# Gated cross-attention block: softmax issued two steps ahead, the work behind it regrouped, and one PSUM tile for each chunk of the first layer

## Chip, cores, metric

One core of one Trainium2 chip. The metric is the device time of one launch in microseconds (us), as the median of several runs.

## What is computed

`x` is 4096 rows of 512 floats. It passes two residual stages.

```
q = layernorm(x) Wq^T + bq          k, v = ctx Wk^T + bk, ctx Wv^T + bv      (ctx: 2 x 77 rows)
a = softmax(q k^T / sqrt(32))       16 heads of 32
x = x + tanh(g0) * (concat(a v) Wo^T + bo)
n = layernorm(x);  h = gelu(quant(n) quant(w1)^T + b1 ...)      512 -> 2048
x = x + tanh(g1) * (quant(h) quant(w2)^T + b2 ...)              2048 -> 512
```

`quant` rounds to whole numbers with one scale for the whole tensor, the largest absolute value over 127. So no row of the first layer can start before every row's second layernorm is known, and no row of the second before every value of `h` is.

## The kernel before

The rows form 8 blocks (`NB`) of 512, each of 4 row tiles of 128. All `x` stays in SBUF (`X[i]`). There are three stages.

**Attention** (lines 409 to 501). Block `i` has 8 steps `s`: a step is one group of four heads (`g = s // 2`) and one half of the rows. The helpers, with the names that the profile shows:

- `project_q` (line 245): 4 matmuls into `pq`; ACT copies to `qT`.
- `softmax` (258): 4 matmuls into `ps` (two row groups of the array side by side); DVE takes the maximum `mx` (276) and subtracts into `e` (280); ACT takes exp (286); DVE sums (288) and inverts (290); POOL multiplies (291).
- `transpose_a` (297): 4 PE transposes of `e` into `pta`; ACT copies to `aT` (305).
- `apply_v` (307): 4 matmuls of 32 columns each into `pc`, side by side in four column groups of the array; ACT copies to `cT` (321).
- `project_o` (323): 4 matmuls into `po` over the four `cT`; DVE adds into `X` (333).
- `norm` and `transpose_x` (222, 229) prepare the next block: `xn` on DVE, `ptx` on PE, `xnT` on ACT.
- `norm2_stats`, `norm2_max` (337, 342): the second layernorm's statistics, and the largest value of a block.
- `weight_step` (386): in blocks 1 to 4, DVE finds the largest weight and quantizes w1 and w2.

In step `s` the code issues the softmax of step `s + 1`, the two transposes of step `s`, and other pieces at fixed steps. Here PE's order isn't written out by hand: a scheduler orders each engine's instructions by its own model of the times, starting from the source, and may put matmuls of one group between those of another. Each engine then runs its list in order, with semaphores between engines. `tc.issue_after` puts a group behind a given instruction; `manual_schedule` keeps the source's order on the engines that it names.

`e` has 3 buffers; `ps`, the transposes' tile `pt` (for `pta` and `ptx`) and the tile `pp` (for `pq`, `pc` and `po`) have 2 each in PSUM.

**Between the stages** (493 to 569). After the last `project_o`, the last tile's layernorm gives the last maximum; `scale_of` (148) turns the maxima into one scale by a small matmul (`pg_x`). Block 0 is normalized for the first layer by POOL (`normalize_x(0, nc.gpsimd)`, line 563, tile `xs`), quantized and transposed through `px` to `xqT`.

**First layer** (570 to 611). Each block has 16 chunks (`fc`) of 128 hidden units, of 4 matmuls each. Two chunks share one PSUM tile `ph` of two banks, and there are two such tiles; the waits go by the tile. ACT applies Gelu to a chunk (590), DVE takes the largest value of two chunks (600). The next block is normalized, quantized and transposed (`xs`, `xq`, `px`, `xqT`) within the same loop. `G` goes to DRAM for six blocks and stays in SBUF for two.

**Second layer** (623 to 665): quantize `G`, 64 matmuls a block into `pf`, add, write out. The change leaves it alone.

Of the kernel before, what the change touches and what calls it, by code (L numbers as in the profile page):

```python
# [8 lines left out]
F32 = mybir.dt.float32  # L9
# [33 lines left out]
def tile_flamingo_gated_block(  # L43
# [50 lines left out]
    bv_sb = awts.tile([NK, D], F32, name="bv_sb")  # L94
# [5 lines left out]
    b2_sb = const.tile([P, D], F32, name="b2_sb")  # L100
# [17 lines left out]
    nc.sync.dma_start(b2_sb, b2.to_broadcast([P, D]))  # L118
# [10 lines left out]
    w1q = const.tile([P, KC, FF], BF16, name="w1q")  # L129
    w2q = const.tile([P, FC, D], BF16, name="w2q")  # L130
# [33 lines left out]

    def quantize(dst, src, inv):
# [8 lines left out]
    with actx:  # L174
        work = actx.enter_context(tc.tile_pool(name="work", bufs=2))
# [4 lines left out]
        kblk, vblk = [], []  # L180
        for b in range(B):
            kb = awts.tile([P, NG, RK], F32, name=f"kb{b}")
            nc.gpsimd.memset(kb, 0.0)
            kblk.append(kb)
            vblk.append(awts.tile([NK, D], F32, name=f"vb{b}"))
# [56 lines left out]
        def add_bias(i, t):  # L242
            nc.gpsimd.tensor_tensor(X[i][:, t, :], X[i][:, t, :], bo_sb, ALU.add)
# [98 lines left out]
        def norm2_max(i, t0=0, t1=NT):  # L342

            tm = small.tile([P, NT], F32, tag="tm", name=f"tm{i}_{t0}")
            for t in range(t0, t1):
                xn = work.tile([P, D], F32, tag="xn", name=f"xf{i}_{t}")
                nc.vector.tensor_scalar(
                    xn,
                    X[i][:, t, :],
                    mean2[:, i, t, 0:1],  # L350
                    rstd2[:, i, t : t + 1],
                    ALU.subtract,
                    ALU.mult,
                )
# [4 lines left out]
            nc.vector.tensor_reduce(xmax[:, k : k + 1], tm[:, : t1 - t0], AX.X, ALU.max)  # L359
# [67 lines left out]
        softmax(0, 0)  # L427
        for i in range(NB):
            for s in range(2 * NG):
                last = None  # L430
                if s + 1 < 2 * NG:
                    last = softmax(i, s + 1)
                    last_product = last["POOL"]
                elif i + 1 < NB:
                    last = softmax(i + 1, 0)
                transpose_a(i, s, 0)

                if i == 0 and s < 2:
# [36 lines left out]
                if s == 7 and i > 0:  # L475
                    norm2_stats(i - 1)
                    norm2_max(i - 1)
                if last is not None:
                    with tc.issue_after(last["DVE"]):
                        weight_step(i, s)  # L480
                    t = s - NT if i == 0 else s // 2
                    if t >= 0 and (i == 0 or s % 2 == 0):
                        with tc.issue_after(last["POOL"]):
                            add_bias(i, t)
# [23 lines left out]
    )  # L508

    def gtile(name):  # L510
        return gpool.tile([P, GF, TB], F32, tag="G", name=name)

# [4 lines left out]
    with ExitStack() as fctx:  # L517
        fwork = fctx.enter_context(tc.tile_pool(name="fwork", bufs=2, reuse_waits="tile"))
        ps_h = fctx.enter_context(
            tc.tile_pool(name="ps_h", bufs=2, space=PSUM, reuse_waits="tile")  # L520
# [5 lines left out]
        def normalize_x(i, engine):  # L526
            xs = fwork.tile([P, NT, D], F32, tag="xs", name=f"xs{i}")
            for t in range(NT):
                engine.tensor_scalar(
                    xs[:, t, :],  # L530
                    X[i][:, t, :],
                    mean2[:, i, t, 0:1],
                    rstd2[:, i, t : t + 1],
                    ALU.subtract,
                    ALU.mult,
                )
            return xs

        def quantize_x(i, xs, n):
# [3 lines left out]
            for t0 in range(0, NT, n):  # L543
                v, vq = xs[:, t0 : t0 + n, :], xq[:, t0 : t0 + n, :]
                if n == 1 and t0 >= NT // 2:
                    nc.scalar.activation(v, v, AF.Copy, bias=MAGIC, scale=inv_x)
                    last = nc.vector.tensor_scalar(vq, v, MAGIC, None, ALU.subtract).ins
                else:
                    last = quantize(vq, v, inv_x)
                for t in range(t0, t0 + n):  # L550
                    px = ps_x.tile([P, KC, P], BF16, tag="px", name=f"px{i}_{t}")
                    for kc in range(KC):
                        nc.tensor.transpose(px[:, kc, :], xq[:, t, kc * P : (kc + 1) * P], identb)
                    dst = xqT[:, :, t * P : (t + 1) * P]
                    if n == 1:
                        nc.scalar.copy(dst, px)  # L556
                    else:
                        nc.vector.tensor_copy(dst, px)
            return xqT, last
# [9 lines left out]
        nc.vector.tensor_scalar(b1s, b1_sb, s1, None, ALU.mult)  # L569
        for i in range(NB):  # L570
            cur = xqT
            if i + 1 < NB:
                with tc.issue_after(last):
                    xs = normalize_x(i + 1, nc.vector)
                xqT, last = quantize_x(i + 1, xs, NT)
            for a in range(GT):
                G = gtile(f"G{i}_{a}")
                for v in range(GF // 2):
                    ph = ps_h.tile([P, 2, TB], F32, tag="ph", name=f"ph{i}_{a}_{v}")
                    for u in range(2):  # L580
                        fc = a * GF + 2 * v + u
                        for kc in range(KC):
                            nc.tensor.matmul(  # L583
                                ph[:, u, :],
# [7 lines left out]
                            ph[:, u, :],  # L592
# [135 lines left out]
```

## Time and profile before

| | |
|---|---|
| median of 3 runs | 720.01 us (718.1 to 720.77) |
| the profiled execution, its own time | 718.17 us |
| its span, first to last instruction | 716.2 us |
| mean granted PE clock | 0.986 of full |
| busy: PE, DVE, ACT, POOL | 662.0, 526.9, 345.7, 210.7 us |
| attention, PE's first `ps` to last `po` | 22.5 to 443.1 us |
| from there to the first matmul of layer one | to 457.6 us |
| layer one, PE | 457.6 to 584.2 us |
| rest | to 716.2 us |

A row of a timeline has a start, a length (both in us from the span's start), the engine, the line, the operation, what it writes and reads, and a count of like instructions merged. In brackets stands how long its engine was idle before it and who ended that. The ends of matmuls are modelled and overlap what follows, so for PE the distance from start to start is the true cost. A float matmul shows as two records.

### The profile page before, as it was taken

To read this page: it belongs to the slowest core of one execution; us is meant where nothing else is said; L and a number is where in the kernel's file an instruction comes from. 1 tells how busy PE (TensorE), PEld (TensorE's weight loads), DVE (VectorE), ACT (ScalarE), POOL (GpSimd) and SP (SyncE) were. 2 spreads that over 40 slices of the span, in tenths; PEclk is the share of its full clock that TensorE was granted. 3 is DMA by queue.
4 is the path that set the end of the run, shared out by engine and by line. 5 is a ranking of instruction groups with operands and counts; after the bars stand their busy time and mean duration, and the time that the engine had idled before them with its cause. 6 is when DMAs were issued, how large, how long until landed. Compare 5 with 4: busy or idle time off the path is not lost.

```text
span 716.2 us, 8398 instructions
## 1 busy us (share of the span) xinstructions
PE 662.0 (92%) x3160; PEld 326.6 (46%) x3160; DVE 526.9 (74%) x821; ACT 345.7 (48%) x474; POOL 210.7 (29%) x164
## 2 busy tenths in 40 slices
PE   4998999899999999999999997699999978999977
PEld 2655445445445445454555543344444433444433
DVE  3564678889888799587577668799997669855542
ACT  2455344334344334444444440477777779454540
POOL 2134323234232342432333232300000009991000
PEclk9999999999999999999999999699999999999999
DMA  9900200121311311100000000066666107699871
GB/s 300 343 1 11 107 0 1 37 82 59 118 59 59 119 59 59 59 1 0 1 1 0 1 1 0 22 271 259 271 265 264 59 0 293 249 346 335 329 253 74
DMA packets 26432, 85.44 MB, mean 119 GB/s; under 512 B 3531, under 2 KB 3531, under 8 KB 20248
## 3 DMA queue, kind: packets, MB, share of 16 engines
q1 hardware_dynamic: 24520, 83.54, 31.0%
q10 hardware_dynamic: 1872, 1.37, 0.6%
q8 instruction: 25, 0.41, 0.2%
q14 instruction: 15, 0.12, 0.0%
HBM read 51.34 MB, written 33.55 MB: 119 GB/s over the span
## 4 chain that ended last, share of the span: by engine, by line
PE 58%; DVE 21%; DMA 7%; POOL 6%; ACT 4%; issue 3%; SPq 1%; POOLq 0%; DVEq 0%; ACTq 0%
PE ph L583 17%; PE pq L248 9%; PE po L326 8%; PE pf L645 7%; PE pta L304 6%; DMA Gb<-h 6%; PE ps L267 4%; POOL e L291 3%; DVE mx L276 3%; PE pc L313 3%; DVE sm L288 2%; DVE e L280 2%; DVE st_a L141 2%; ACT Gb L636 1%; DVE st_f L141 1%
## 5 line engine op out<-in xcount | busy, mean ns | idle before, releaser
L291 POOL TENSOR_TENSOR e<-e,rs 128x616 f32<-128x616 f32 x64 | 77.9, 1218 | 261.7 <-DVE rs L290 190.2
L583 PE MATMUL ph<-xqT,w1q 128*128 128x512 bf16 x512 | 124.2, 381 | 0.9 <-ACT xqT L556 0.7
L645 PE MATMUL pf<-w2q,hq 128*128 128x512 bf16 x512 | 114.4, 386 | 9.4 <-DVE hq L637 4.9
L248 PE MATMUL pq<-xnT,wq_sb 128*128 128x512 f32 x256 | 121.0, 613 | 0.9 <-ACT xnT L240 0.9
L305 ACT COPY aT<-pta 77x512 f32<-77x512 f32 x128 | 73.5, 580 | 93.7 <-PE pta L304 93.6
L326 PE MATMUL po<-wo_sb,cT 128*128 128x512 f32 x256 | 117.5, 597 | 0.0
L590 ACT ACTIVATE G<-ph,b1s,s 128x512 f32<-128x512 f32 x128 | 99.5, 777 | 28.9 <-PE ph L583 23.8
L659 POOL TENSOR_TENSOR x<-x,b_sb 128x512 f32<-128x512 f32 x32 | 57.9, 1853 | 135.6 <-DVE b_sb L616 135.6
L304 PE MATMUL pta<-ident,e 128*77 128x128 f32 x512 | 81.2, 284 | 13.8 <-POOL e L291 11.0
L304 PEld LDWEIGHTS pta<-ident,e 128*77 128x77 f32 x512 | 57.7, 147 | 68.1 <-POOL e L291 33.7
L600 DVE TENSOR_REDUCE hmax<-G 128x1 f32<-128x1024 f32 (+1 forms) x65 | 75.2, 1196 | 16.4 <-ACT G L590 16.1
L645 PEld LDWEIGHTS <-hq 128*128 128x128 bf16 x512 | 50.4, 99 | 73.2 <-issue 8.3
L583 PEld LDWEIGHTS <-w1q 128*128 128x128 bf16 x512 | 49.2, 97 | 67.6 <-issue 18.2
L276 DVE TENSOR_REDUCE mx<-ps 128x8 f32<-128x616 f32 x64 | 50.2, 786 | 39.9 <-PE ps L267 39.6
L248 PEld LDWEIGHTS pq<-xnT,wq_sb 128*128 128x128 f32 x256 | 46.7, 194 | 53.2 <-issue 50.2
L636 ACT ACTIVATE Gb<-Gb,inv_h 128x2048 f32<-128x2048 f32 x24 | 47.6, 1999 | 46.3 <-DMA Gb<-h 46.3
L288 DVE TENSOR_REDUCE sm<-e 128x8 f32<-128x616 f32 x64 | 50.4, 789 | 25.0 <-ACT e L286 24.4
L286 ACT ACTIVATE e<-e 128x616 f32<-128x616 f32 x64 | 45.8, 716 | 42.6 <-DVE e L280 42.5
L326 PEld LDWEIGHTS po<-wo_sb,cT 128*128 128x128 f32 x256 | 45.6, 190 | 45.0 <-issue 44.5
L637 DVE TENSOR_SCALAR hq<-Gb 128x2048 bf16<-128x2048 f32 x24 | 36.9, 1547 | 32.2 <-ACT Gb L636 32.2
L267 PE MATMUL ps<-kb,qT 64*128 64x154 f32 x512 | 55.5, 319 | 0.9 <-ACT qT L256 0.8
L256 ACT ACTIVATE qT<-pq,bq_sb 128x512 f32<-128x512 f32 x32 | 22.0, 687 | 65.5 <-PE pq L248 65.5
(90 smaller groups left out, 646.5 us busy)
## 6 DMA issues: line engine op xcount, KB each, us to landing
h<-G SPq DMA_DIRECT2D x24, 1024.0 KB, 3.8
Gb<-h SPq DMA_DIRECT2D x24, 1024.0 KB, 7.2
raw_w<-in_w2T SPq DMA_DIRECT2D x8, 1024.0 KB, 5.0
out_y<-x SPq DMA_DIRECT2D x32, 256.0 KB, 3.8
x<-in_x SPq DMA_DIRECT2D x7, 1024.0 KB, 5.0
raw_w<-in_w1T SPq DMA_DIRECT2D x4, 1024.0 KB, 9.8
x<-in_x SPq DMA_DIRECT2D x4, 256.0 KB, 6.2
wq_sb<-in_wqT ACTq DMA_DIRECT2D x1, 1024.0 KB, 10.6
```

The costliest lines, as they stand in the source:

```text
L248: nc.tensor.matmul(pq, wq_sb[:, kc, g * P : (g + 1) * P], xnT[i][:, kc, :], start=(kc == 0), stop=(kc == KC - 1),)
L267: nc.tensor.matmul(ps[:, q, u * RK : (u + 1) * RK], qT[i, g][r, t * P : (t + 1) * P], kblk[i // NBB][r, g, :], start=True, stop=True,)
L276: nc.vector.tensor_reduce(mx, sc, AX.X, ALU.max)
L288: nc.vector.tensor_reduce(sm, e4, AX.X, ALU.add)
L291: last["POOL"] = nc.gpsimd.tensor_tensor(e4, e4, rs[:, :, :, None].to_broadcast([P, 2, HG, NK]), ALU.mult).ins
L304: nc.tensor.transpose(pt[:NK, j, :], es[i, s][:, u, j, :], ident)
L305: nc.scalar.copy(aT[i, g][:, :, t * P : (t + 1) * P], pt[:NK, :, :])
L326: nc.tensor.matmul(po, cT[i, g][:, t * P : (t + 1) * P], wo_sb[:, g, :], start=(g == 0), stop=(g == NG - 1),)
L583: nc.tensor.matmul(ph[:, u, :], w1q[:, kc, fc * P : (fc + 1) * P], cur[:, kc, :], start=(kc == 0), stop=(kc == KC - 1),)
L590: nc.scalar.activation(G[:, 2 * v + u, :], ph[:, u, :], AF.Gelu, bias=b1s[:, fc : fc + 1], scale=s1,)
L600: nc.vector.tensor_reduce(hmax[:, k + u : k + u + 1], G[:, 2 * v + u : 2 * v + u + n, :], AX.XY, ALU.max, apply_absolute_value=True,)
L645: nc.tensor.matmul(po[t], hq[:, fc, t * P : (t + 1) * P], w2q[:, fc, :], start=(fc == 0), stop=(fc == FC - 1),)
```

## The change

- The softmax is issued two steps ahead in place of one: two softmaxes and one more `project_q` before the loop, and step `s` issues that of `s + 2`.
- The pieces of a step stand at other steps. `apply_v` of the group before and `project_o` of the block before come at even steps, one behind the other (before: 2, 4, 6, 0 and 1, 3, 5, 6). `project_q` comes at 1 and 3 for the groups 2 and 3, and at 5 and 7 for groups 0 and 1 of the next block. `norm` goes from step 3 to step 1, `transpose_x` from 5 and 6 to 3 and 5.
- Block 0's normalization for the first layer moves from POOL, after the attention, to DVE in step 5 of the last block (`xs0`, in a buffer of `aT`). Its quantization and transposition stand in the attention's pools (`xq0`, `xqT0`), with two of the four copies on DVE. The last tile's `norm2_max` is kept behind the one before it.
- First layer: each chunk has its own `ph` of one bank, with four of them, and PE keeps the source's order. The 16 transposes of the next block's `xq` stand together ahead of the last four chunks of a block.
- The load of `b2` moves from the start to after the attention; `bv_sb` moves to a buffer of `cT`.

```diff
-        softmax(0, 0)
+        softmax(0, 0)
+        softmax(0, 1)
+        project_q(0, 1)
         for i in range(NB):
             for s in range(2 * NG):
-                last = None
-                if s + 1 < 2 * NG:
-                    last = softmax(i, s + 1)
-                    last_product = last["POOL"]
+                if s + 2 < 2 * NG:
+                    last = softmax(i, s + 2)
                 elif i + 1 < NB:
-                    last = softmax(i + 1, 0)
+                    last = softmax(i + 1, s + 2 - 2 * NG)
                 transpose_a(i, s, 0)
...
-                if s == 0:
-                    if i > 0:
-                        apply_v(i - 1, NG - 1)
-                    project_q(i, 1)
...
-                if s in (2, 4):
-                    project_q(i, 1 + s // 2)
-                    apply_v(i, s // 2 - 1)
-                if s in (1, 3, 5, 6) and i > 0:
-                    project_o(i - 1, (1, 3, 5, 6).index(s))
-                if s == 6:
-                    apply_v(i, 2)
+                if s % 2 == 0:
+                    if s > 0:
+                        apply_v(i, s // 2 - 1)
+                    elif i > 0:
+                        apply_v(i - 1, NG - 1)
+                    if i > 0:
+                        project_o(i - 1, s // 2)
+                if s in (1, 3):
+                    project_q(i, (s + 3) // 2)
                 if i + 1 < NB:
-                    if s == 3:
+                    if s == 1:
                         with tc.issue_after(last["DVE"]):
                             norm(i + 1)
-                    if s in (5, 6):
-                        for t in (2 * s - 10, 2 * s - 9):
+                    if s in (3, 5):
+                        for t in (s - 3, s - 2):
                             transpose_x(i + 1, t)
                 transpose_a(i, s, 1)
-                if s == 6 and i + 1 < NB:
-                    project_q(i + 1, 0)
+                if s in (5, 7) and i + 1 < NB:
+                    project_q(i + 1, (s - 5) // 2)
...
+                with tc.issue_after(last["DVE"]):
+                    weight_step(i, s)
+                    if i == NB - 1 and s == 5:
+                        xs0 = work.tile([P, NT, D], F32, tag="aT", name="xs0", bufs=3)
+                        for t in range(NT):
+                            normalize2(xs0[:, t, :], 0, t)
...
-                    norm2_max(NB - 1, t - 1, t)
-        norm2_max(NB - 1, NT - 1, NT)
+                    last = norm2_max(NB - 1, t - 1, t)
+        with tc.issue_after(last):
+            norm2_max(NB - 1, NT - 1, NT)
+        s_x, inv_x = scale_of(xmax, "x", ps_p, "pp")
+        xq0 = work.tile([P, NT, D], BF16, tag="xnT", name="xq0", bufs=1)
+        for t in range(NT):
+            v, vq = xs0[:, t, :], xq0[:, t, :]
+            if t < NT // 2:
+                with tc.issue_after(last):
+                    last = quantize(vq, v, inv_x)
+            else:
+                nc.scalar.activation(v, v, AF.Copy, bias=MAGIC, scale=inv_x)
+                last = nc.vector.tensor_scalar(vq, v, MAGIC, None, ALU.subtract).ins
+        for t in range(NT):
+            px = ps_t.tile([P, KC, P], BF16, tag="pt", name=f"px0_{t}")
+            transpose_q(px, xq0[:, t, :])
+            copy = nc.vector.tensor_copy if t % 2 else nc.scalar.copy
+            copy(xqT0[:, :, t * P : (t + 1) * P], px)
...
-            tc.tile_pool(name="ps_h", bufs=2, space=PSUM, reuse_waits="tile")
+            tc.tile_pool(name="ps_h", bufs=4, space=PSUM, reuse_waits="tile")
...
-        with tc.issue_after(last_product), tc.high_priority(offset=300):
-            xs = normalize_x(0, nc.gpsimd)
-        s_x, inv_x = scale_of(xmax, "x", ps_g, "pg")
-        xqT, last = quantize_x(0, xs, 1)
+        def quantize_x(i):
+            xs = fwork.tile([P, NT, D], F32, tag="xs", name=f"xs{i}")
+            xq = fwork.tile([P, NT, D], BF16, tag="xq", name=f"xq{i}")
+            xqT = fwork.tile([P, KC, TB], BF16, tag="xqT", name=f"xqT{i}")
+            for t in range(NT):
+                normalize2(xs[:, t, :], i, t)
+            quantize(xq, xs, inv_x)
+            return xq, xqT
+
+        def transpose_xq(i, xq, xqT):
+            for t in range(NT):
+                px = ps_x.tile([P, KC, P], BF16, tag="px", name=f"px{i}_{t}")
+                transpose_q(px, xq[:, t, :])
+                nc.vector.tensor_copy(xqT[:, :, t * P : (t + 1) * P], px)
...
+        fctx.enter_context(tc.manual_schedule(engines={mybir.EngineType.PE}))
         for i in range(NB):
-            cur = xqT
+            cur = xqT if i else xqT0
             if i + 1 < NB:
                 with tc.issue_after(last):
-                    xs = normalize_x(i + 1, nc.vector)
-                xqT, last = quantize_x(i + 1, xs, NT)
+                    xq, xqT = quantize_x(i + 1)
             for a in range(GT):
                 G = gtile(f"G{i}_{a}")
+                if a == GT - 1 and i + 1 < NB:
+                    transpose_xq(i + 1, xq, xqT)
                 for v in range(GF // 2):
-                    ph = ps_h.tile([P, 2, TB], F32, tag="ph", name=f"ph{i}_{a}_{v}")
                     for u in range(2):
                         fc = a * GF + 2 * v + u
+                        ph = ps_h.tile([P, TB], F32, tag="ph", name=f"ph{i}_{fc}")
```

`normalize2` is the one DVE instruction that `normalize_x` had (subtract the mean, multiply by the inverse deviation); `transpose_q` is the four transposes of one row tile.

More of the change, by code (lines that the diff above doesn't have):

```diff
@@ L93, in tile_flamingo_gated_block @@
     ctx_sb = awts.tile([P, B, KC, NK], F32, name="ctx_sb")
-    bv_sb = awts.tile([NK, D], F32, name="bv_sb")
+    kblk = [awts.tile([P, NG, RK], F32, name=f"kb{b}") for b in range(B)]
+    vblk = [awts.tile([NK, D], F32, name=f"vb{b}") for b in range(B)]
+    work = actx.enter_context(tc.tile_pool(name="work", bufs=2))
+    bv_sb = work.tile([NK, D], F32, tag="cT", name="bv_sb", bufs=7)
     bq_sb = const.tile([P, KC], F32, name="bq_sb")
@@ L99, in tile_flamingo_gated_block @@
     b1_sb = const.tile([P, FC], F32, name="b1_sb")
-    b2_sb = const.tile([P, D], F32, name="b2_sb")
     load_x(0, pieces=NT)
@@ L117, in tile_flamingo_gated_block @@
     nc.sync.dma_start(b1_sb, b1)
-    nc.sync.dma_start(b2_sb, b2.to_broadcast([P, D]))
     ident = const.tile([P, P], F32, name="ident")
@@ L129, in tile_flamingo_gated_block @@
     w1q = const.tile([P, KC, FF], BF16, name="w1q")
+    xqT0 = const.tile([P, KC, TB], BF16, name="xqT0")
     w2q = const.tile([P, FC, D], BF16, name="w2q")
@@ L163, in scale_of, with normalize2, transpose_q @@
         return s, inv
+    def normalize2(dst, i, t):
+        nc.vector.tensor_scalar(
+            dst,
+            X[i][:, t, :],
+            mean2[:, i, t, 0:1],
+            rstd2[:, i, t : t + 1],
+            ALU.subtract,
+            ALU.mult,
+        )
+    def transpose_q(dst, src):
+        for kc in range(KC):
+            nc.tensor.transpose(dst[:, kc, :], src[:, kc * P : (kc + 1) * P], identb)
     def quantize(dst, src, inv):
@@ L174, in tile_flamingo_gated_block @@
     with actx:
-        work = actx.enter_context(tc.tile_pool(name="work", bufs=2))
         ps_s = actx.enter_context(tc.tile_pool(name="ps_s", bufs=2, space=PSUM))
@@ L178, in tile_flamingo_gated_block @@
         ps_p = actx.enter_context(tc.tile_pool(name="ps_p", bufs=2, space=PSUM))
-        kblk, vblk = [], []
-        for b in range(B):
-            kb = awts.tile([P, NG, RK], F32, name=f"kb{b}")
+        for kb in kblk:
             nc.gpsimd.memset(kb, 0.0)
-            kblk.append(kb)
-            vblk.append(awts.tile([NK, D], F32, name=f"vb{b}"))
         def project_k(b, g):
@@ L346, in norm2_max @@
                 xn = work.tile([P, D], F32, tag="xn", name=f"xf{i}_{t}")
[L347 to L354, printed above, removed]
+                normalize2(xn, i, t)
                 nc.vector.tensor_reduce(
@@ L358, in norm2_max @@
             k = i if t1 - t0 == NT else NB - 1 + t0
-            nc.vector.tensor_reduce(xmax[:, k : k + 1], tm[:, : t1 - t0], AX.X, ALU.max)
+            return nc.vector.tensor_reduce(
+                xmax[:, k : k + 1], tm[:, : t1 - t0], AX.X, ALU.max
+            ).ins
         wraw, wmax = {}, {}
@@ L477, in tile_flamingo_gated_block @@
                     norm2_max(i - 1)
[L478 to L484, printed above, removed]
+                with tc.issue_after(last["DVE"]):
[4 more added lines that the diff above has]
+                            normalize2(xs0[:, t, :], 0, t)
+                t = s - NT if i == 0 else s // 2
+                if t >= 0 and (i == 0 or s % 2 == 0):
+                    with tc.issue_after(last["POOL"]):
+                        add_bias(i, t)
             if i + 2 < NB:
@@ L508, in tile_flamingo_gated_block @@
     )
+    late = ctx.enter_context(tc.tile_pool(name="late", bufs=1, reuse_waits="tile"))
+    b2_sb = late.tile([P, D], F32, name="b2_sb")
+    nc.sync.dma_start(b2_sb, b2.to_broadcast([P, D]))
     def gtile(name):
@@ L524, in tile_flamingo_gated_block @@
         )
-        def normalize_x(i, engine):
+        def quantize_x(i):
             xs = fwork.tile([P, NT, D], F32, tag="xs", name=f"xs{i}")
[L528 to L539, printed above, removed]
             xq = fwork.tile([P, NT, D], BF16, tag="xq", name=f"xq{i}")
             xqT = fwork.tile([P, KC, TB], BF16, tag="xqT", name=f"xqT{i}")
[L543 to L559, printed above, removed]
-        with tc.issue_after(last_product), tc.high_priority(offset=300):
-            xs = normalize_x(0, nc.gpsimd)
-        s_x, inv_x = scale_of(xmax, "x", ps_g, "pg")
-        xqT, last = quantize_x(0, xs, 1)
+            for t in range(NT):
[7 more added lines that the diff above has]
+                nc.vector.tensor_copy(xqT[:, :, t * P : (t + 1) * P], px)
         s1 = const.tile([P, 1], F32, name="s1")
@@ L569, in tile_flamingo_gated_block @@
         nc.vector.tensor_scalar(b1s, b1_sb, s1, None, ALU.mult)
+        fctx.enter_context(tc.manual_schedule(engines={mybir.EngineType.PE}))
         for i in range(NB):
-            cur = xqT
+            cur = xqT if i else xqT0
             if i + 1 < NB:
                 with tc.issue_after(last):
-                    xs = normalize_x(i + 1, nc.vector)
-                xqT, last = quantize_x(i + 1, xs, NT)
+                    xq, xqT = quantize_x(i + 1)
             for a in range(GT):
                 G = gtile(f"G{i}_{a}")
+                if a == GT - 1 and i + 1 < NB:
+                    transpose_xq(i + 1, xq, xqT)
                 for v in range(GF // 2):
-                    ph = ps_h.tile([P, 2, TB], F32, tag="ph", name=f"ph{i}_{a}_{v}")
                     for u in range(2):
                         fc = a * GF + 2 * v + u
+                        ph = ps_h.tile([P, TB], F32, tag="ph", name=f"ph{i}_{fc}")
                         for kc in range(KC):
                             nc.tensor.matmul(
-                                ph[:, u, :],
+                                ph,
                                 w1q[:, kc, fc * P : (fc + 1) * P],
@@ L591, in tile_flamingo_gated_block @@
                             G[:, 2 * v + u, :],
-                            ph[:, u, :],
+                            ph,
                             AF.Gelu,
```

## Prediction

> **What bounds the kernel now.** I read the page first, then the busy times of four stretches, the waits of the attention, and the timelines of PE, DVE and ACT inside each stage. The page says that PE is it:
>
> ```profile
> PE 662.0 (92%) x3160; PEld 326.6 (46%) x3160; DVE 526.9 (74%) x821; ACT 345.7 (48%) x474; POOL 210.7 (29%) x164
> ```
>
> PE's share is an average of stages with different limits. The stretches are attention, transition, first layer and rest (columns: busy us of PE, its weight loads, DVE, ACT, POOL; granted clock; DMA):
>
> ```profile
> 69.00:429.00 360.00, 346.75 (x1688) 178.25 (x1686) 280.06 (x487) 149.78 (x252) 120.74 (x98) 1.00 0.12 42
> 443.20:457.60 14.40, 2.94 (x19) 2.25 (x20) 10.84 (x27) 3.48 (x6) 9.43 (x5) 0.62 0.00 0
> 457.60:584.30 126.70, 126.45 (x622) 55.71 (x622) 109.32 (x130) 97.96 (x127) 0.00 (x0) 0.99 0.49 199
> ```
>
> So attention is PE with some 13 us of holes, the transition a chain with PE nearly idle, the first layer again PE, with DVE at 86%. In attention one wait leads, the transposes of `e` on POOL's product:
>
> ```profile
> POOL e L291 <- DVE rs L290: 190.2, 41, 17.1
> ...
> PE pta L304 <- POOL e L291: 11.0, 18, 1.5
> ```
>
> That 11.0 us is what a softmax two steps ahead can remove. PE's timeline of block 5 shows what its order costs (the first `ps` is cut in two around a transpose):
>
> ```profile
> 316.44 3.60 PE L326 MATMUL po<-wo_sb,cT 128*128 128x512 f32 x8
> 319.88 1.04 PE L239 MATMUL ptx<-ident,xn 128*128 128x128 f32 x8
> 320.84 0.53 PE L267 MATMUL ps<-kb,qT 64*128 64x154 f32 x2
> 321.30 0.66 PE L304 MATMUL pta<-ident,e 128*77 128x128 f32 x4
> 321.89 0.79 PE L267 MATMUL ps<-kb,qT 64*128 64x154 f32 x6
> 322.61 0.66 PE L304 MATMUL pta<-ident,e 128*77 128x128 f32 x4
> ```
>
> From start to start a whole `ps` takes 0.72; here one of its four matmuls alone takes 0.46 and the other three still 0.72. They run side by side, so a cut adds 0.46. In the transition POOL's normalization is last, and DVE's next step beside it takes 1.00 where the same step takes 0.54 a tile earlier:
>
> ```profile
> 444.95 0.54 DVE L347 TENSOR_SCALAR xf<-x,mean,rstd 128x512 f32<-128x512 f32 x1
> ...
> 445.89 8.66 POOL L529 TENSOR_SCALAR xs<-x,mean,rstd 128x512 f32<-128x512 f32 x4
> 445.93 1.00 DVE L347 TENSOR_SCALAR xf<-x,mean,rstd 128x512 f32<-128x512 f32 x1 [0.43 <-POOL rstd L145]
> ```
>
> In the first layer the chain gives 8 matmuls 1.89 us, where they take 1.73 when nothing holds them:
>
> ```profile
> 472.86 1.89 PE ph L583 x8
> 474.75 0.45 PE px L553 x8
> 475.19 1.73 PE ph L583 x8
> ```
>
> The scheduler alternates two `ph` tiles chunk by chunk. A tile's second chunk waits for the Gelu of its first, since waits go by the tile: 0.2 to ACT's start and 0.78 for Gelu, 1.03 in all, while one chunk of the other tile covers 0.86. That is 0.165 for 8 matmuls, and such gaps occur 49 times: 8.1 us.
>
> [...] here, after the transition, the first matmuls of layer one come 0.43 us apart in place of 0.216. [...]
>
> **Attention.** The 11.0 us on `e` go: in the new order 6 us and more of PE work lie between a softmax's issue and its former need, and DVE's weight steps (1.2 to 1.8 us each) no longer reach PE. Next late is PE's own work. The changed program's order cuts 13 of the 32 `pc` groups into one matmul and three, with a `ps` between, where before none was cut. Records of 512 columns come 0.43 apart (`pq`: 8 in 3.44). A `pc` group takes 1.0, its four matmuls being side by side; one alone takes two records, 0.86, and with the change of shape 0.97. Lower bound of a cut 0, if it only fills PE's wait for `qT`; upper 1.0, the whole group again. I take 0.97, since `ps` shows the full price, and count no wait for `qT` there. In return `pq` and `po` are no longer cut, and `ps` less often.
>
> One block is then: 16 `pta` of 0.53 = 8.5; 8 `pq` and `po` of 3.47 = 27.8; `ps` 7 of 0.73 and two halves of 0.46 = 6.0; `pc` 2 of 1.0 and 2 of 1.97 = 5.9; `ptx` 1.9; a cut `pta` 0.2. Sum 50.3. New waits: `ptx` and `pta` now follow in a row through two PSUM buffers that ACT empties in 0.58 each, 0.5. So 50.8. (The same sum for block 6 before: `pc` 4.0, `ps` 6.3, 48.7, and 1.0 of waits: 49.7, against 49.95 in the trace.)
>
> Block by block, from the start of `pq` for group 1 (76.3, 127.5, 180.5, 232.3, 284.9, 336.7, 386.6 us), six blocks took 310.3. They will take 6 x 50.8, plus 2.5 for the weight steps' lag and the two `pg_w` matmuls: 307.3, so -3.0. Block 0: at its start PE waits for `qT` 0.8, later for `e` and `aT` 2.5; summed in the new order from `ps` at 22.5, with `pk` 0.9, `pvv` 3.44 and the prices above, that `pq` starts at 71.3, with one `pc` (1.0) still to do: -4. The last block has a cut `pc` more and 0.8 of waits less: 0. DVE's four `xs0` (4 x 0.5) lie there under 6.5 us of PE work ahead of the last softmax's transposes; uncovered they cost 2. **Attention: -7**, from -19 (cuts free) to 0. The moved loads (`b2`, 0.25 MB on SP's queue, last of the start, now ahead of the `h` stores, needed 130 us later) cost nothing.
>
> **Transition.** After the last `po` (443.15): add 0.75, statistics to 445.1, POOL's power 0.78 to 445.9. Meanwhile tile 2's `xf`, `tm`, `xmax` run (to 446.3), then tile 3's 0.54 + 0.69 + 0.15 to 447.7. Maximum to scale took 448.33 to 450.39, so the scale is there at 449.8. DVE needs about 0.45 for each of 6 quantizing steps and 0.2 for `b1s`: 452.7, ACT's two (0.72) beside them. Then the last transposes at half clock, 0.2 wait and 0.43, wait and copy 0.6, matmul at 454.6, against 457.57. **-3.0**, from -2 to -5. [...]
>
> **First layer.** The 49 holes go: -8.1. But the 16 transposes now stand together in PE's list. `px` has two buffers, so the third waits for DVE's first copy, the fourth for the second, and the block's last four chunks wait behind them. On DVE's list in four of seven blocks the maximum of chunks 10 and 11 stands ahead of the second copy. From T, the end of chunk 11: Gelu at T+0.2 to T+1.0, maximum 1.2 (2.34 for two) to T+2.25, copy 0.41, transposes: chunk 12 starts at T+2.98, where T+0.87 would do. That is 2.1. DVE has 8 x 1.13 + 4 x 0.5 + 2.33 + 4 x 0.34 = 14.7 a block, so in blocks 1 to 3 it comes to this point late. Block 1: the fourth copy ends at T+4.5; then stand two quantizing steps (1.2, 1.13), six maxima (6.8) and `xs` (2.5 to 3), some 12.7 us, so the maximum of chunks 8 and 9 starts at T+17.2, while chunk 11 ends at T' = T+2.98 + 16 x 0.863 = T+16.8. From T'+0.4 follow that maximum 1.13, the first copy 0.35, the next maximum 1.13 and the second copy 0.41: chunk 12 at T'+3.75, 2.9 late. Blocks 2 and 3 the same way: 3.1 and 2.9. In blocks 4, 5, 6 both copies come first: 0.75 each. Sum +13.2 (bounds 4 to 20). At the end only one chunk's Gelu and a half maximum follow PE, not two: -0.9. **First layer: +4.2.**
>
> **Sum.** -7 - 3.0 + 4.2 = -5.8 on the profiled execution's 718.17: 712.4. The median shown is 1.84 above that execution, so 714.2.
>
> **Rivals.**
> - *The attention gains nothing*: ACT's list becomes the bound (an exp waiting for DVE with copies behind it, while PE has two buffers). For: copies of `pta` end most of ACT's waits. Against: ACT is at 42%. 714.2 + 7 = 721.2. Chance 0.22.
> - *The cuts are free*: for: a `ps` needs `qT` about then. Against: the price of the cut `ps`. 13 x 0.97 = 12.6 less: 701.6. Chance 0.13.
> - *Slower: [...].* In blocks 0 to 3 of the first layer the transposes' stall, at about 3 us, [...] each then also starts its chunks at half clock, 2.1 us as after the transition. 4 x 2.5 = 10: 724.2. [...] Against: a hole of 2.6 us at 606 us doesn't slow PE. Chance 0.13.
> - My forecast: 0.52.
>
> **From cases to numbers.** About 0.5% (3.6 us) is what a measurement tells from no change. Below 716.4 lie the free cuts and three quarters of my own case (its stage errors make about 4 us): 0.52. Above 723.6 most of the slower rival: 0.14. The rest, 0.34, is no change. As faster and not faster are near even, the likeliest case's own range is 710 to 718. The range for 8 in 10 is 704 to 724, with about 0.1 left out at each end.
>
> **What would show it.** `pta`'s waits on POOL near 0; `pc` rows of two and six records, 1.97 a pair; blocks of some 51 us; 11.5 us from the last `po` to the first `ph`; in the first layer no holes of 0.165, but 2 to 3 us at the `px` of blocks 0 to 3 and under 1 later, ended by DVE's copies. Wrong would be: uncut blocks near 49, no stall at `px`, or half-speed matmuls after it.

## The result, and the profile after

The changed kernel takes 709.69 us (median of 4, 707.17 to 710.06), the kernel before 719.06 (median of 4, 714.94 to 720.77): ratio 0.987, 95% interval 0.982 to 0.992. (The medians leave out executions that took over 1.5% longer than the fastest of the same kernel, which happened to one kernel only, in five of 14.) The profiled execution of the changed kernel took 710.06 us, its span 707.9. Forecast were 714.2 and a range of 704 to 724.

The page's line of busy times, of the changed kernel:

```profile
PE 659.4 (93%) x3138; PEld 331.4 (47%) x3160; DVE 529.1 (75%) x827; ACT 342.9 (48%) x472; POOL 200.8 (28%) x160
```

By this line PE's idle time fell from 54.2 to 48.5 us, and its busy time by 2.6 (22 matmul records are missing from this trace). The share of busy time doesn't tell where the 8.3 us of the span come from, so each stage is looked at by itself. The same stretches as before (busy us of PE, weight loads, DVE, ACT, POOL; granted clock; DMA), cut at this kernel's own borders:

```profile
69.00:425.00 356.00, 351.04 (x1671) 181.09 (x1671) 277.46 (x485) 147.26 (x250) 119.24 (x99) 1.00 0.11 41
438.40:449.20 10.80, 3.02 (x18) 2.03 (x18) 8.49 (x26) 2.51 (x4) 0.78 (x1) 0.65 0.00 0
449.20:580.70 131.50, 121.07 (x612) 57.60 (x624) 112.20 (x133) 98.70 (x127) 0.00 (x0) 0.98 0.47 192
580.70:707.90 127.20, 114.10 (x505) 50.75 (x514) 80.85 (x77) 63.18 (x34) 57.90 (x32) 0.97 0.71 264
```

In the attention PE is now busy for 351 of 356 us. In the first layer it was busy for 126.45 of 126.70 and is now idle for 10 of 131.5; the old holes of 0.165 us lie inside what counts as busy, so only times from start to start show that they went. The stages, cut at the end of the last `po`, the first `ph`, the matmul `pg_h` (which spreads the largest value of `h`, so the first layer is over) and the end of the span:

| stage | before | after | difference |
|---|---|---|---|
| start to the end of the last `po` | 443.1 | 438.1 | -5.0 |
| to the first `ph` | 14.5 | 11.1 | -3.4 |
| to `pg_h`, so with the end of the first layer | 129.9 | 133.8 | +3.8 |
| to the end | 128.7 | 124.9 | -3.8 |

Of the attention's -5.0, 0.3 is a first `ps` that came earlier (22.15 instead of 22.45 us). From the first `ps` to the end of the last `po` it went from 420.66 to 415.98, so -4.7. This distance repeats: all three profiles with the old attention, and all seven with the new one, agree within 0.05 us.

POOL's wait for DVE is as long as before. Over the whole span it is 190.0 us, where 190.2 stood, and in the middle of the attention (69 to 429 us before, 69 to 425 after):

```profile
POOL e L291 <- DVE rs L290: 161.0, 37, 11.6
```

```profile
POOL e L303 <- DVE rs L302: 166.2, 38, 8.4
```

What changed is that PE no longer stands behind it: its waits for POOL, 9.7 us in this stretch before, are gone from it. The idle time of an engine that isn't the bound was not the loss. PE's order there is the one foreseen, a `pc` cut around a `ps`:

```profile
331.66 0.60 PE L316 MATMUL pta<-ident,e 128*77 128x128 f32 x4
332.19 1.05 PE L325 MATMUL pc<-aT,vb 77*32 77x512 f32 x2
333.16 0.80 PE L279 MATMUL ps<-kb,qT 64*128 64x154 f32 x8
333.89 1.06 PE L325 MATMUL pc<-aT,vb 77*32 77x512 f32 x6
334.88 3.70 PE L338 MATMUL po<-wo_sb,cT 128*128 128x512 f32 x8
```

From start to start the lone product takes 0.97 and the other three 0.99. The next table, of PE's waits over the whole span, has the first layer's new stall in its second row:

```profile
PE ptx L251 <- DVE xn L246: 9.9, 3, 6.2
PE px L180 <- DVE xqT L569: 9.6, 10, 2.6
PE pg_x L158 <- DVE diag_x L156: 5.2, 1, 5.2
```

The first row lies at the kernel's start. The second is ten waits in seven blocks. PE's timeline shows those of blocks 2 and 3:

```profile
494.99 0.61 PE L180 MATMUL px<-identb,xq 128*128 128x128 bf16 x8
498.17 0.71 PE L180 MATMUL px<-identb,xq 128*128 128x128 bf16 x8 [2.56 <-DVE xqT L569]
498.72 13.98 PE L590 MATMUL ph<-xqT,w1q 128*128 128x512 bf16 x62
512.53 0.61 PE L180 MATMUL px<-identb,xq 128*128 128x128 bf16 x8
514.21 0.38 PE L180 MATMUL px<-identb,xq 128*128 128x128 bf16 x4 [1.07 <-DVE xqT L569]
515.67 0.38 PE L180 MATMUL px<-identb,xq 128*128 128x128 bf16 x4 [1.07 <-DVE xqT L569]
```

Sixteen transposes without a stall take 0.87, so block 2 lost 498.72 - 494.99 - 0.87 = 2.86. Between the stalls nothing is lost: the 64 matmuls of 16 chunks (two records are missing) take 512.53 - 498.72 = 13.81 us, 0.216 each. After block 3's stalls the clock dropped (the last columns are granted clock, DMA share and GB/s):

```profile
498.00:512.00 14.00, 13.73 (x68) 6.56 (x70) 13.96 (x20) 11.02 (x15) 0.00 (x0) 1.00 0.55 225
512.00:516.00 4.00, 1.85 (x21) 1.26 (x19) 3.95 (x6) 1.43 (x2) 0.00 (x0) 1.00 0.77 315
516.00:532.00 16.00, 15.95 (x72) 7.10 (x71) 10.20 (x10) 12.07 (x16) 0.00 (x0) 0.89 0.52 212
```

0.11 of 16 us is about 1.8 us of work lost. Read in steps of half a microsecond, the clock stands at half from 516.7 for 3.4 us, so 1.7 us. From 498 to 516 DVE is busy throughout (17.91 of 18 us), and the copies stand behind its other work: the first of block 3 starts at 513.75, behind two maxima that began at 511.49. And 3.8 us came from the second layer, where neither an instruction nor its order was changed. That was not forecast.

### The profile page after: what moved, and what is told of

It is laid out like the page before. It is cut to its first block, busy times and chain, and to the rows that moved or that the text cites. A ratio compares the mean times of both kernels' runs of the same rounds, so it can differ in the third digit from the quotient of the medians.

```text
span 707.9 us, 8370 instructions
## 1 busy us (share of the span) xinstructions
PE 659.4 (93%) x3138; PEld 331.4 (47%) x3160; DVE 529.1 (75%) x827; ACT 342.9 (48%) x472; POOL 200.8 (28%) x160
## 3 DMA queue, kind: packets, MB, share of 16 engines
q10 hardware_dynamic: 1872, 1.37, 0.7%
## 4 chain that ended last, share of the span: by engine, by line
PE 70%; DVE 16%; DMA 7%; ACT 4%; issue 1%; SPq 1%; POOL 0%; ACTq 0%; DVEq 0%
PE po L338 15%; PE pq L260 15%; PE ph L590 9%; PE pta L316 8%; PE pf L652 7%; PE ps L279 6%; DMA Gb<-h 6%; PE pc L325 6%; DVE hmax L607 5%; PE ptx L251 2%; DVE xs L169 1%; ACT Gb L643 1%; DMA x<-in_x 1%; DVE xs L184 1%; PE pvv L223 1%
## 5 line engine op out<-in xcount | busy, mean ns | idle before, releaser
L260 PE MATMUL pq<-xnT,wq_sb 128*128 128x512 f32 x256 | 117.8, 603 | 2.0 <-ACT xnT L252 2.0
L590 PE MATMUL ph<-xqT,w1q 128*128 128x512 bf16 x500 | 114.0, 386 | 1.3 <-DVE xqT L526 0.5
L607 DVE TENSOR_REDUCE hmax<-G 128x1 f32<-128x1024 f32 (+1 forms) x65 | 77.4, 1200 | 19.1 <-ACT G L597 19.0
L316 PE MATMUL pta<-ident,e 128*77 128x128 f32 x512 | 79.3, 280 | 1.7 <-ACT aT L317 1.2
L316 PEld LDWEIGHTS pta<-ident,e 128*77 128x77 f32 x512 | 59.8, 147 | 40.6 <-issue 34.3
L292 DVE TENSOR_TENSOR e<-ps,mx 128x616 f32<-128x616 f32 x64 | 50.9, 796 | 2.9
L279 PE MATMUL ps<-kb,qT 64*128 64x154 f32 x512 | 52.7, 319 | 0.2
```

Of the source, the lines that this page charges most:

```text
L260: nc.tensor.matmul(pq, wq_sb[:, kc, g * P : (g + 1) * P], xnT[i][:, kc, :], start=(kc == 0), stop=(kc == KC - 1),)
L279: nc.tensor.matmul(ps[:, q, u * RK : (u + 1) * RK], qT[i, g][r, t * P : (t + 1) * P], kblk[i // NBB][r, g, :], start=True, stop=True,)
L316: nc.tensor.transpose(pt[:NK, j, :], es[i, s][:, u, j, :], ident)
L590: nc.tensor.matmul(ph, w1q[:, kc, fc * P : (fc + 1) * P], cur[:, kc, :], start=(kc == 0), stop=(kc == KC - 1),)
L607: nc.vector.tensor_reduce(hmax[:, k + u : k + u + 1], G[:, 2 * v + u : 2 * v + u + n, :], AX.XY, ALU.max, apply_absolute_value=True,)
```

## Experiments

All are the changed kernel with an edit, unless said otherwise. "First layer" in this part is the time from the first `ph` to `pg_h`.

**The transposes spread.**

```diff
-                if a == GT - 1 and i + 1 < NB:
-                    transpose_xq(i + 1, xq, xqT)
...
+                        if i + 1 < NB and FC - 6 <= fc < FC - 2:
+                            transpose_xq(i + 1, xq, xqT, fc - FC + 6)
```

> The changed kernel with one edit: the next block's four transposes go one each ahead of chunks 10 to 13 instead of all four ahead of chunk 12. Theory A (the four in a row stall PE, because px has two buffers and the DVE copies lie behind maxima that wait for Gelus): the 11.8 us of stalls at px, and with them the 1.7 us that PE lost to a lower clock after the longest of them, go; the first layer falls from 131.4 us to about 118 and the kernel from 709.7 us to about 696. Theory B (DVE, which is busy 10 to 14 us of every 14 to 17 there, sets the pace; the copies come as late as before, and PE then waits at the next block's first product): less than half is gained, 703 us or more.

Measured: 700.43 us, ratio to the kernel before 0.976 (0.973 to 0.979). First layer 123.2 instead of 133.8. Of ten waits two are left, 1.36 us in block 2 and 0.53 in block 3. The first layer gained 10.6 of the 13.5 expected, 1.9 of the rest being these waits. Theory A: the stall is the price of standing together; DVE has the same instructions as before, and from 460 to 560 us PE is now busy for 98.1 of 100 us, where it was for 90.2 (DVE 94.4 and 87.2). (Two of the four also come one and two chunks earlier; no run separates that.) PE's timeline of block 2, where 2.56 stood:

```profile
488.72 0.39 PE L180 MATMUL px<-identb,xq 128*128 128x128 bf16 x4
488.94 1.03 PE L589 MATMUL ph<-xqT,w1q 128*128 128x512 bf16 x4
489.81 0.39 PE L180 MATMUL px<-identb,xq 128*128 128x128 bf16 x4
490.03 1.03 PE L589 MATMUL ph<-xqT,w1q 128*128 128x512 bf16 x4
492.42 0.38 PE L180 MATMUL px<-identb,xq 128*128 128x128 bf16 x4 [1.36 <-DVE xqT L568]
```

**Own tiles, the planner's order.** The line with `manual_schedule` for PE in the first layer is taken out.

> The changed kernel with one edit: own PSUM tile for each chunk kept, but the first layer in the planner's order instead of the source's. Theory A (own tiles take away the 0.165 us holes whatever the order; the source's order brings the stalls): the planner splits the third and fourth px from the first two by 3 to 6 products, so about 9 to 12 of the 11.8 us of stalls go and no hole comes back: first layer 119 to 122 us, kernel 697 to 700. Theory C (the holes went because PE follows the source, not because of the tile): some 49 holes of 0.165 us come back, +8.1, and the kernel is near 706.

Measured: 704.82 us. First layer 123.1, with 1.3 us of waits at `px`, and no holes: 62 matmuls of `ph` in a row took 13.38 us from start to start, 0.216 each. So the tile, not the order, took the holes away. The total missed the expected 697 to 700: the second layer took 131.8 us in its profile, the longest of all, where the changed kernel's took 124.9.

**The first layer as before**: that edit, and the shared tile of two banks again (`ps_h` with two buffers, `ph[:, u, :]`).

> The changed kernel with the first layer as before: one PSUM tile of two banks for two chunks and the planner's order. Theory A (the first layer's two edits together cost +4.7 us and gave 0.9 back at its end): first layer near 126.7 us again with some 49 holes, kernel near 706. Rival D (the first layer's part is a gain that the profile's stage table hides, for example in the second layer, which ended 3.8 us earlier): kernel at 713 to 718.

Measured: 711.75 us. First layer 132.0, 9.0 more than with own tiles in the same kind of order. Its chain has the holes again:

```profile
466.92 1.90 PE ph L589 x8
468.82 0.00 issue
468.83 1.89 PE ph L589 x8
470.71 0.00 issue
```

One stall of 1.5 us at the end of block 0 is new. The expected 706 was missed by 5.7, 4.8 of it in the second layer (129.7 against 124.9 us). The first layer's two edits, then, are a gain of about 9 (the tiles) and a loss of about 10 (the transposes together, by the first experiment), and the second layer's time had to be settled by itself.

**The kernel before with own tiles alone.**

```diff
-                    ph = ps_h.tile([P, 2, TB], F32, tag="ph", name=f"ph{i}_{a}_{v}")
+                        ph = ps_h.tile([P, TB], F32, tag="ph", name=f"ph{i}_{fc}")
```

> The kernel before with one edit: each chunk of the first layer in its own PSUM tile of one bank, four of them, the order left to the planner. Theory A (49 holes of 0.165 us come from two chunks sharing a tile): -8.1, and -0.9 at the last chunk: 718.8 falls to about 710. Rival C (the holes come from the planner's order, and own tiles alone remove none, or the planner reorders px so that new stalls take the gain): 715 or more.

Measured: 710.74 us (0.991, 0.988 to 0.994). First layer 124.5 instead of 129.9, though PE ran at half clock for its first 5.6 us in that execution and for 2.6 us before, some 1.5 us of work. Theory A, and by its ratio this one edit is worth nearly as much as the whole change (0.987).

**The output's stores on GpSimd's queue.**

```diff
-            nc.sync.dma_start(out[r : r + P, :], y)
+            queue = nc.sync if i == first - 1 else nc.gpsimd
+            queue.dma_start(out[r : r + P, :], y)
```

> The changed kernel with one edit in the second layer: the stores of the output go through GpSimd's queue (the last block's stay on SP's), so that a load of h never lies behind a store that waits for the last product of a block. Theory F (the part of the gain that was not predicted, 3.8 us from the scale of h to the end, is how late the loads come in one execution, which varies from 124.9 to 131.8 us between profiles with the same instructions): the waits of PE for hq go, the stretch falls to 121 to 123 us, and the kernel to 704 to 707. Rival G (the loads are held by the DMA engines' own rate, not by SP's order): the waits stay, the kernel is within 2 us of 709.7 or slower.

Measured: 705.19 us (704.52 to 706.02). From `pg_h` to the end 122.1 us. First the end of the second layer in the changed kernel, then in this one:

```profile
603.97 85.63 PE L652 MATMUL pf<-w2q,hq 128*128 128x512 bf16 x388 [1.05 <-DVE x L670]
692.26 11.40 PE L652 MATMUL pf<-w2q,hq 128*128 128x512 bf16 x51 [2.66 <-DVE hq L644]
```

```profile
602.81 96.85 PE L652 MATMUL pf<-w2q,hq 128*128 128x512 bf16 x439 [1.64 <-DVE x L670]
```

The hole before the last block is gone: theory F. In the changed kernel SP (SyncE) stood for 83.7 us before stores whose row tile DVE hadn't finished, with the next block's loads behind them in its list. The waits of SP's list there, from 580 us on:

```profile
SPq L672 <- DVE x L670: 83.7, 28, 8.0
```

What decided here is that the loads stood behind these waits: with the stores out of SP's list the hole of 2.66 us is gone, and that was worth 2.8 us in the second layer. Of the 4.5 between the medians, another 1.2 lies in the first layer of the profiles, where this execution had no drop of the clock (1.00 granted from 460 to 580 us).

**The kernel before with the same edit.**

> The kernel before with one edit: the output's stores on GpSimd's queue. Theory F (the second layer's stretch is the same in both kernels, about 122 us when no load lies behind a store; what it was beyond that in each profile is chance): 128.7 falls to 122 to 123, kernel near 712, and the changed kernel with the same edit (705.2) stands 6 to 8 us below it, which is what the change itself is worth by its stages: -4.7, -3.6, +4.7, -0.9 = -4.5, and up to 2 more. Rival L (the change makes the second layer shorter by itself): the stretch here stays above 125 us, kernel 715 or more.

Measured: 711.31 us (711.26 to 713.25), from `pg_h` to the end 122.1 us. Rival L falls. The pair gives the change's own worth without the second layer's variation: 711.31 to 705.19, -6.1 us. By the stages of the table above, in their profiles: -4.5, -3.4, +2.5, 0.0; sum -5.4, which is the difference of the spans (709.3 and 703.9). What makes the unedited second layer 124.9 us in one kernel and 131.8 in another, when the stores stand ahead of the loads, stays open.

**One buffer for `px`**, with the stores on GpSimd's queue (705.19 without it).

> The changed kernel with the output's stores on GpSimd's queue (705.2 us) and one edit in the first layer: one buffer for px instead of two, so that the second px of each block waits for the first copy too. Theory A (PE waits for the DVE copies one by one, so the stall grows with each buffer taken away): one more stall of 0.6 to 1.3 us in each of 7 blocks, +4 to +9, kernel 709 to 714; if the stalls of a block then reach the lower clock oftener, up to +1.7 more for each of the first four. Rival K (the last copy of a block is what counts, and it comes when DVE gets to it, whatever the number of buffers): the stall is only moved, within 2 us of 705.2.

Measured: 720.01 us, +14.8. First layer 147.2 against 132.6. PE's waits at `px` are 18.5 us, in 21 pieces, where 9.6 in 10 stood: the stall grows when a buffer is taken away, so theory A, and K falls. That explains 8.9 of 14.6; three drops of the clock (0.91 granted in three stretches of 20 us), at 1.7 each, explain 5.1 more, and 0.6 is left. PE's timeline of block 0, then the clock after it:

```profile
459.44 0.39 PE L180 MATMUL px<-identb,xq 128*128 128x128 bf16 x4
460.64 0.39 PE L180 MATMUL px<-identb,xq 128*128 128x128 bf16 x4 [0.81 <-DVE xqT L569]
462.09 0.38 PE L180 MATMUL px<-identb,xq 128*128 128x128 bf16 x4 [1.07 <-DVE xqT L569]
463.62 0.38 PE L180 MATMUL px<-identb,xq 128*128 128x128 bf16 x4 [1.14 <-DVE xqT L569]
463.84 0.47 PE L590 MATMUL ph<-xqT,w1q 128*128 128x512 bf16 x1
```

```profile
465.00:470.00 5.00, 5.00 (x19) 2.01 (x18) 3.71 (x7) 3.11 (x4) 0.00 (x0) 0.76 0.00 0
```

No wait at `px` in this layer is above 1.33 us, and the clock falls all the same. From the last `ph` ahead of these transposes to the next one stand 4.4 us (459.44 to 463.84), in which PE did nothing but sixteen transposes. What in these 4.4 us lowered the clock, no run shows.

**PE's order written out in the attention**, with `apply_v` ahead of the next softmax at every even step, in a `manual_schedule` for PE.

> The changed kernel with PE's order in the attention written out: apply_v ahead of the next softmax's products, so that none of the 13 groups of pc is cut. Theory A (a cut costs 0.97 us, because its lone product takes as long as all four, and nothing else waits): 13 cuts go, a block of the attention falls from 51.05 us by 1.5 to 2, the kernel from 709.7 us to about 697. Rival E (with the products of the scores later by one pc, e comes too late again, and PE waits at pta for POOL as it did before the change): waits of 1 us and more at pta come back, and less than 4 us is gained, 706 us or more.

Measured: 721.66 us, 12 us slower than the changed kernel. No `pc` is cut, and the last `po` comes 7.7 us later. PE's waits in the attention:

```profile
PE pg_w L158 <- DVE diag_w L156: 6.5, 2, 3.2
PE pta L316 <- ACT xnT L252: 5.2, 12, 1.0
PE pc L325 <- ACT aT L317: 5.0, 10, 1.2
PE ps L279 <- ACT qT L268: 3.8, 6, 0.6
PE pta L316 <- POOL e L303: 1.8, 2, 0.9
```

With a smaller row that is 22.5 us of waits, where the changed kernel has 4.8 in this stretch: 17.7 more. The lower clock after the second wait at `pg_w` (0.93 granted from 227 to 279 us) adds some 3.4. Against them stand the 12.6 of cuts; that makes 8.5, and from the first `ps` to the last `po` it measures 8.4. So the sum comes out if the cuts gave back their price, and the new waits cost more. Neither theory named the largest: `pg_w` now stands where the source has it, ahead of its operand. The edit moved more than `pc`: at steps 2 and 4, where none had been cut, it put two `pta` in a row and `ps` behind `pc`.

**The same, the order left to the planner.**

> The changed kernel with apply_v traced ahead of the next softmax, and the order of the attention left to the planner: no group of pc is cut any more, some groups of the scores' products (ps) are cut instead, and the scale of the weights is placed by the planner again. Theory A (the cuts of pc are the loss, 0.97 us each): 13 cuts of pc go, -12.6 us; a ps cut in two measured 0.92 against 0.72 us in the changed kernel, so some 15 cuts of ps give back 3; the last po comes 9 us earlier and the kernel is near 700. Theory E2 (what the whole-group kernel before this one showed: with pc moved, PE waits for ACT's copies aT, xnT and qT, 14 us in all there): the cuts go and the waits come, the attention ends within 3 us of the changed kernel's, kernel 707 to 713.

Measured: 716.83 us, 7 above the changed kernel and above what both theories gave. Its profiled execution took 722.77 us, so only its parts are read, and where the 7 us lie is not shown. The last `po` comes 4.0 us later, 3.4 of it from two drops of PE's clock (0.97 granted in two stretches of 52 us); PE waits 6.3 us for `qT` and 4.1 at `pg_w`. Without the drops the attention is as in E2: the cuts go, and waits of the same size come.

**`pc` whole, all else in place.** Only at the steps 0 and 6 is the softmax issued behind `apply_v`. The stores are on GpSimd's queue.

```diff
+                first_v = s % 6 == 0
+                if not first_v:
+                    last = next_softmax(i, s)
                 transpose_a(i, s, 0)
...
+                if first_v:
+                    last = next_softmax(i, s) or last
```

> The changed kernel with the output's stores on GpSimd's queue (705.2 us measured, with little spread), and one edit in the attention: at steps 0 and 6 of a block the next softmax is traced behind apply_v. The order of PE is then that of the changed kernel but for the 13 cut groups of pc, which run whole ahead of the same ps, and the order of VectorE, ScalarE and GpSimd is kept. Theory A (a cut costs 0.97 us and nothing hangs on it): ps starts 0.02 us later than behind the lone product, -12.6 us, kernel near 692.6. Theory E (the lone product fills a wait for an ACT copy or for e, which shows as soon as it goes, as in the two kernels in which pc was moved before): less than 5 us is gained, 700 or more.

Measured: 697.92 us against 705.19, so -7.3, between the two theories. The expectation's theory A holds for some blocks and fails for others. From one `pq` of group 1 to the next (us), with the mended order from the kernel of the next experiment, whose profile has no lower clock in the attention:

| block | 1 | 2 | 3 | 4 | 5 | 6 |
|---|---|---|---|---|---|---|
| changed kernel | 51.05 | 52.15 | 51.05 | 52.15 | 51.04 | 51.05 |
| `pc` whole | 49.10 | 51.26 | 49.99 | 51.25 | 49.56 | 49.11 |

Blocks 1 and 6 gain 1.95, two cuts at 0.97. In blocks 2 to 4, which have steps for the weights, DVE is busy for 43 to 45 of 50 to 52 us (36 to 38 in the others; block 1 has such steps too), and some 1 us of each block's gain is lost again. PE's timeline of the kernel with `pc` whole at the first of them:

```profile
130.53 0.66 PE L316 MATMUL pta<-ident,e 128*77 128x128 f32 x4
132.56 0.34 PE L316 MATMUL pta<-ident,e 128*77 128x128 f32 x1 [1.37 <-ACT aT L317]
133.12 0.49 PE L158 MATMUL pg_w<-diag_w,ones 128*128 128x128 f32 x2 [0.22 <-DVE diag_w L156]
133.44 5.30 PE L260 MATMUL pq<-xnT,wq_sb 128*128 128x512 f32 x8
```

and the waits between 125 and 140 us in it:

```profile
ACT e L298 <- DVE e L292: 5.6, 1, 5.6
```

A transpose waits 1.37 us for a PSUM buffer that ACT is to empty, and ACT's copy stands behind an exp that waited 5.6 us for DVE. That is the prediction's rival of ACT's list. In the next experiment's kernel blocks 2 and 4 both have this wait, 1.4 us each; block 3 has 0.5 of `ps` waiting for `qT` instead, and block 5 0.2, so that the 0.5 which block 5 loses isn't explained. In the rows above `pq` then takes 5.1 us in place of 3.4, at the lower clock (0.83 granted from 130 to 140 us).

**The three mends together**: stores, whole `pc`, spread `px`.

> The three mends together: stores of the output on GpSimd's queue, pc whole, px spread over chunks 10 to 13. Theory A (the three are independent, since they lie in different stages): 705.2 - 12.6 - 9.3 = 683 us. If pc whole gains nothing: 696. If the gains meet one limit, as an engine other than PE that becomes the bound in the first layer: 688 or more while the kernel with pc whole alone is at 693.

Measured: 688.33 us (687.85 to 688.69), 0.959 of the kernel before (0.956 to 0.963): the best of all. It is 9.6 below the kernel with whole `pc` alone, so the first layer's gain (9.3 expected) adds in full. Of the 5.3 us that miss from 683, the table shows 3.0 in blocks 2 to 4 and 0.5 in block 5; the rest was not located.

**The stage between, as before**: normalized by GpSimd in the first layer's pools, transposed one by one, copied by ACT.

> The changed kernel with the stage between the attention and the first layer as it was: the first block is normalized on GpSimd in the first layer's pools, piecewise quantized and copied by ACT, after these pools open. Theory A (this part is worth what the stage table shows, 14.4 us down to 10.8): +3.6, kernel near 713. Rival H (the stage is bound by the last block's own chain of statistics and maximum, so the placement of the first block's normalizing is worth nothing): within 1 us of 709.7.

Measured: 715.33 us, +5.6. The stage took 14.5 us, +3.4 as the table of stages says: theory A. The total is above the 713 expected mainly because the second layer, which the edit doesn't touch, took 129.1 us in this profile and not 124.9.

## Why the prediction was right, and where it was off

The direction and the sum held: -5.8 was forecast, and the pair with the stores moved shows -6.1. That the sum is this close is partly luck: the attention gained 2.3 us less than forecast, and the first layer lost 1.7 less. The point of 714.2 lies 4.5 above the median, for two reasons that come below. Step by step:

- **The waits for `e` go**: right, none is left in this stretch. **A cut costs 0.97**: right in the profile (0.97, against 1.00 for a whole group), and blocks 1 and 6 give back just that when it is mended. The rival "the cuts are free" is wrong.
- **A block is 50.8, and six take 307.3**: 308.5 measured. The new wait of `ptx`, `pta` and `pq` for ACT's copies is 0.7 a block, not 0.5. Instead of -3.0 the six blocks gave -1.8.
- **Block 0, `pq` at 71.3**: 70.8 measured, 0.3 of the difference from the earlier first `ps`; without it block 0 gives -4.2, with -4 forecast. **The last block 0**: it took 58.9 us, and 56.5 before. One moved `pc` (1.0) belongs to that, so +1.4: the further cut costs 0.97, a wait for ACT's copy 0.3, and no waits went. **Attention -7**: -4.7 from the first `ps` on. The mechanism was right, the size a third off, and the missing 2.3 are 1.2 in the six blocks and 1.4 in the last, less 0.2 that block 0 gave beyond its forecast. No run separates the softmax two steps ahead from the regrouped work behind it, so what each of them gave is not shown.
- **Transition -3.0**: -3.4 measured, and the old stage alone costs 3.4 again.
- **First layer, holes -8.1**: right. They are gone in every kernel with own tiles, whichever the order; the two tile forms in the planner's order stand 9.0 us apart. **Stalls +13.2**: 2.0, 2.7, 2.9, 2.5 and three times 0.6, which is 11.8. In six of the seven blocks the copies and maxima came in the order foreseen; in block 2 both copies came together behind two maxima. The 2.9 of block 1 is partly luck: its list of DVE's work is put at 12.7 us, but its items make 11.6 to 12.1, with which the stall would have come out nearer 2. **-0.9 at the end**: from the end of the last `ph` to `pg_h` 2.58 us became 2.32, so -0.3 (the last `ph` before ends at 584.9, not at the 584.2 of the table of times). The terms as measured make +3.4. The pair shows +2.5, so 0.9 belongs to none of them; the changed kernel's own profile shows +3.8, with one drop of the clock (1.7) in it.
- **Second layer 0**: right for the change itself, and yet the largest miss in the time shown. The 3.8 us belong to the loads behind waiting stores, not to the change; with the stores on another queue both kernels take 122.1.
- **The median 1.84 above the profiled execution**: this was added for the changed kernel too, but its median lies 0.37 below. So 714.2 - 709.7 = 4.5 comes from the second layer (3.8) and this (2.2), less the 1.2 by which the other stages gained less and some rounding.
- **The slower rival** went by the length of one stall, an estimate that no trace of before showed, and put the half clock after the transition at 2.1 us. In that profile it ends at 460.2, 2.6 us after the first `ph`, so 1.3 us of work. The length of one stall is the wrong measure: the clock fell after block 3, whose two waits were 1.07 each, and not after block 2, whose one was 2.56; with one buffer it fell three times after waits of at most 1.33. In the kernel with PE's order written out two waits at `pg_w` were alike, and the clock fell at the second only (in the two stretches around them the granted clock, third from the end, is 1.00 and then 0.93):

```profile
135.31 0.46 PE L158 MATMUL pg_w<-diag_w,ones 128*128 128x128 f32 x2 [3.23 <-DVE diag_w L156]
240.63 0.77 PE L158 MATMUL pg_w<-diag_w,ones 128*128 128x128 f32 x2 [3.22 <-DVE diag_w L156]
```

```profile
123.00:175.00 52.00, 47.03 (x238) 25.10 (x237) 46.12 (x78) 20.41 (x35) 16.02 (x14) 1.00 0.17 61
227.00:279.00 52.00, 47.03 (x218) 24.93 (x217) 43.87 (x74) 19.32 (x33) 15.63 (x13) 0.93 0.21 77
```

Equal stalls drop the clock in one execution and not in another: the kernel with only the stores moved has the same `px` waits, 9.6 us, and no drop in the first layer. Each drop read in the first layers lasted 3.4 us at half clock, and the one at `pg_w`, worked out from the 0.93 over 52 us, about twice that. What sets a drop off, no run shows.

## What to carry to other kernels

Ask of each half of an edit what it is worth alone: here one PSUM tile for each chunk was worth 7 to 9 us, and an order that came with it cost 10. When a chain of waits is removed on the bound engine, look at what the scheduler puts in its place: here a group of four small matmuls that run side by side (1.00 us) was cut, at 0.97 a cut, and it was mended by moving one neighbour, and not by writing out the whole order. Where two kernels differ by less than a stage varies, remove that variation first; then a difference of 6 us in 700 is plain.

## What was not expected of the hardware

- PE's clock fell after short waits in a row: 0.81, 1.07 and 1.14 us within 4.4 us, and the half clock that followed for 3.4 us cost 1.7. It doesn't always: the same waits at `px`, 9.6 us in ten, brought one drop in the changed kernel's profile and none in that of the kernel with only the stores moved.
- Loads that stand behind waiting stores in one engine's list of transfers made the second layer 124.9 to 131.8 us long in kernels with the same instructions there. With the stores on GpSimd's queue five profiles gave 122.0 to 122.1.
- A lone product of four that otherwise run side by side takes as long as all four, 0.97 against 1.00 us.
